# An attention and mixture-of-experts block on one core: rows turned by TensorE in place of DMA transposes, and the diagonal's mask added by VectorE in half of the tiles

## The chip, the core and the metric

The kernel runs on one core of a Trainium2 chip. The metric is the time of one execution on the device in microseconds (us), the median of several runs. TensorE is called PE in the profile, VectorE DVE, ScalarE ACT, GpSimd POOL, and the engine that mostly issues DMAs SP. "Turning" a block of rows is transposing it, so that features lie on partitions, as a matrix product needs them.

## What is computed

The reference takes x of 2 sequences of 2048 tokens with 256 features. All in f32:

```python
mod = silu(c) @ wmod                                  # sa, ca, ga, sb, cb, gb of each sequence
h = layernorm(x) * (1 + ca) + sa
q, k, v = h @ Wq.T, h @ Wk.T, h @ Wv.T                # 2 query heads of 128, one head of keys and values
q, k = apply_rope(q), apply_rope(k)
scores = where(causal, q @ k.T * 128 ** -0.5, -inf)
x = x + ga * ((softmax(scores) @ v) @ Wo.T)           # ga, gb kept away from zero
h = layernorm(x) * (1 + cb) + sb
gate = softmax(h @ Wg + bg); thr = sigmoid(h @ Wt + bt) * 0.125
w = relu(gate - thr); w = w / sum(w)                  # weights of 8 experts
out = x + gb * sum_e w[e] * (gelu(h @ W1[e] + b1[e]) @ W2[e] + b2[e])
```

A token goes only to the experts whose weight is not zero, so how many tokens an expert gets depends on the data.

## The kernel before, in words

**Attention.** The 4096 tokens are 32 tiles of 128 (`tile_steps`), 16 of each sequence, taken in groups of 4, later 2 and 1, from both sequences in turn; r is the tile's number in this order. A tile is loaded (line 505), normalized (516), turned on PE (`turn`, 525), projected to q, k and v (548, 553) and rotated. `score` (600) multiplies a head's q by the keys in chunks of up to 512 columns; the last chunk holds the diagonal, and a second, bf16 product (604) of an identity and a triangular mask is added to it in PSUM. `keep` (611) is one VectorE pass that scales the chunk into SBUF and takes each row's maximum on the way; `top` (618) takes the maximum over the chunks. ScalarE takes the exponentials (627). The probabilities are turned on PE (`turn_p`, ptr, 673), copied out by ScalarE (677) and multiplied by v (pav, 683). After the output projection (717) and the residual sum, `hx` is the second normalization's result. GpSimd splits each f32 of hx into two halves of 16 bits (`halves`, 750), SP writes them to the DRAM table `feats` (759), and in all but the last 4 tiles SP turns them by a DMA transpose of 16-bit elements (`turn_halves`, 771), after which GpSimd or VectorE joins the halves again (`join_halves`, 775). In the last 4 tiles PE turns hx (`turn_h`, 767). A product with the router's weights (787) gives the logits; `gate_steps` forms the weights and the place of each token in its experts' lists.

**The order of attention.** `Plan` holds every step with an engine, an estimated cost, what it comes after, which buffers it takes and gives, and a rank. It plays the steps through and emits each engine's instructions in the order that results. The first steps of a tile (up to the maxima, `lead`) have a rank that is 5 tiles ahead. Each change of a cost, a step or a buffer count can so change the order of all engines. At the start PE runs 8 idle products (312), and `by_feature` (379) makes the shifts and scales of the first normalization by 8 small products.

**Ahead of the experts.** The first 2 items of expert 0 (512 rows) are computed inside attention (1055, 1072, 1079), their rows gathered and turned by `fetch`. Engines then read the token counts into registers (`hold`), PE runs 5 idle products and, behind a barrier, 4 more (1294).

**Experts.** An item is up to 256 tokens of one expert; the last item of an expert can be a half of 128. Items are numbered by t through all experts. Each engine runs its own loop, and semaphores tie them together:

- GpSimd (`item`, 1453): waits until the row buffer xr is free, copies the indices (1441), gathers the item's rows of `feats` by two indirect DMAs (1397); in up to 8 items of an expert it also writes a part of the next expert's list by four indirect DMAs (1413 to 1421); then it adds an earlier item's output to the result by two (1431).
- SP (`turn`, 1233 to 1239): waits for the gather and for xp to be free, and turns xr into xp by one DMA transpose.
- VectorE (`item`, 1338): forms gates, waits until all of item t's h is done, joins xp into xT for item t+1 (`ready`, 1335), adds b2 to y (1363), multiplies by the gate (1374).
- PE (`item`, 1264): waits for xT, makes h in 8 products of two halves each (1272) through HB = 6 PSUM buffers, then y from the 8 gelus (1282).
- ScalarE takes the gelu of each h (1307); at the start of expert e it issues the loads of expert e+2's weights.

b2 of all experts is broadcast to every partition in attention (344).

Of the kernel before, what the change touches and what calls it, by code (L numbers as in the profile page):

```python
# [15 lines left out]
U16 = mybir.dt.uint16  # L16
# [25 lines left out]
HB = 6  # L42
# [68 lines left out]
def adaln_block_kernel(ctx, tc, x, wqkvT, woT, wgt, bgt, w1, b1T, w2, b2, cT, wmod, rope, out):  # L111
# [21 lines left out]

# [16 lines left out]
    b2_bc = const.tile([P, E, D], F32, name="b2_bc")  # L152
    gb_bc = const.tile([P, B, D], F32, name="gb_bc")
    lists = [dram.tile([NTOK, ENT], F32, name=f"list_{e}") for e in range(E)]
    feats = dram.tile([NTOK, 2 * D], U16, name="feats")
# [11 lines left out]
    with tc.manual_schedule():  # L167
        attention(
            tc, x, wqkvT, woT, wgt, bgt, w1, b1T, w2, b2, cT, wmod, rope, out, ident, counts,
            b1_sb, b2_bc, gb_bc, lists, feats, place, entry, weights, wpool,  # L170
            kept,
        )
# [4 lines left out]
    for e in range(RES, E):  # L177
# [3 lines left out]
    xr = ep.tile([P, CI * 2 * D], U16, name="xr")  # L181
    xp = ep.tile([P, CI * 2 * KD, P], U16, name="xp")
# [10 lines left out]
    mcur = ep.tile([P, CI, ENT], F32, name="mcur")  # L193
    to = ep.tile([P, NW], I32, name="to")
    new = ep.tile([P, NW, ENT], F32, name="new")
    hs = [pp.tile([P, TI], F32, name=f"h{z}") for z in range(HB)]
    ys = [pp.tile([P, D], F32, name=f"y{c}") for c in range(CI)]
    experts(
        tc, nc, lists, feats, out.rearrange("b t d -> (b t) d"), counts, ident, b1_sb, b2_bc,
        gb_bc, w1, w2, weights, xr, xp, kept, gs, gate, part, yb, yo_end, who_end, sheets, at, mcur, to, new,  # L200
# [4 lines left out]
def attention(  # L205
    tc, x, wqkvT, woT, wgt, bgt, w1, b1T, w2, b2, cT, wmod, rope, out, ident, counts,
    b1_sb, b2_bc, gb_bc, lists, feats, place, entry, weights, wpool,
# [6 lines left out]
    room = {"ps": 6, "pav": 2, "x": 9, "s": 16, "pT": 3, "hx": 4, "hp": 3, "qT": 3, "big": 3, "xn": 3,  # L214
            "hT": 2, "hT2": 2, "hpT": 2, "aT": 2, "g_sb": 1, "sign": 1, "size": 1}
# [61 lines left out]
    make_causal_mask(nc, maskb, mask_val=MASKED)  # L277
    make_identity(nc, identb)
# [15 lines left out]
    def places_back():  # L294
        nc.vector.tensor_copy(back[:, 0, :], ids)
        for z in (1, 0):
            nc.vector.tensor_scalar(back[:, z, :], back[:, 0, :], float(z - NTOK), None, ALU.add)
# [4 lines left out]
    def load(dst, src, kb, rank=first, **how):  # L302
        return plan.add(
            "SP", max(0.5, kb / 360.0), lambda: nc.sync.dma_start(dst, src), late=2.0, rank=rank,
            **how
        )
# [7 lines left out]
    plan.add("PE", 3.4, lambda: idle_work(8), take=["ps"], give=["ps"], rank=first - 5)  # L314
# [13 lines left out]
    for t0, t1 in [(0, 1), (1, 4)] + [(q, q + 4) for q in range(4, NT, 4)]:  # L328
# [14 lines left out]
    l_b2 = load(  # L343
        b2_bc.rearrange("p e d -> p (e d)"), b2.rearrange("e d -> (e d)").partition_broadcast(P),
        1024, rank=6.0,
    )
# [27 lines left out]

    def by_feature():
        box["pm"] = pm = ps_tile("pm")
        for j in range(2 * KD):
            for k in range(KD):
                nc.tensor.matmul(
                    pm[:, j * B : (j + 1) * B], wm_0[:, k, ts(j, P)], sc[:, k, :],  # L380
                    start=(k == 0), stop=(k == KD - 1),
                )
# [9 lines left out]
    m_pe = plan.add("PE", 2.0, by_feature, after=[s_sc, l_m0], take=["ps"], rank=first)  # L392
# [95 lines left out]
    def tile_steps(b, i, r, group, g):  # L488
# [14 lines left out]
        def load_x():  # L503
# [6 lines left out]
            "SP", 0.5, load_x, late=2.0, take=["x"], rank=first + early[r] if r in early else r  # L510
# [85 lines left out]
        def score(h, c):  # L596
            w = min(SC, n - c * SC)
            st["sc", h, c] = ps = ps_tile(f"psc{u}_{h}_{c}")
            last = c == nch - 1
# [6 lines left out]
        def keep(h, c):  # L606
            w = min(SC, n - c * SC)
            s = st["s", h, c] = work([P, SC], "s", f"{u}_{h}_{c}")
            if ("mx", h) not in st:
                st["mx", h] = little([P, 4], "mx", f"{u}_{h}")  # L610
            nc.vector.tensor_scalar(  # L611
                s[:, :w], st["sc", h, c][:, :w], scale, None, ALU.mult, ALU.max,
                accum_out=st["mx", h][:, c : c + 1],
            )

        def top(h):
            st["nmx", h] = little([P, 1], "nmx", f"{u}_{h}")
            nc.vector.tensor_reduce(  # L618
                st["nmx", h], st["mx", h][:, :nch], AX.X, ALU.max, negate=True
            )  # L620
# [14 lines left out]
        for h in range(NH):  # L635
            kept = []
            for c in range(nch):
                w = min(SC, n - c * SC)
                n_s = lead(
                    "PE", w * 0.00168 + (0.06 if c == nch - 1 else 0.0),  # L640
# [5 lines left out]
                    lead("DVE", 0.1 + w * 0.0013, lambda h=h, c=c: keep(h, c), [n_s], give=["ps"])  # L646
# [101 lines left out]
        def halves():  # L748
            st["hp"] = work([P, 2, D], "hp", u, U16)
            nc.gpsimd.tensor_copy(  # L750
                st["hp"], st["hx"].bitcast(U16).rearrange("p (d two) -> p two d", two=2)
            )


        by_dma = r < NTOK // P - 4
        n_f = add("POOL", 0.65, halves, [n_h], take=["hp"], give=["hx"] if by_dma else [])
        n_hp = add(
            "SP", 0.5,
            lambda: nc.sync.dma_start(
                feats[ts(b * NT + i, P), :], st["hp"].rearrange("p two d -> p (two d)")  # L760
            ), [n_f], late=2.0, give=[] if by_dma else ["hp"],
        )
# [6 lines left out]
        def turn_halves():  # L769
            st["hpT"] = work([P, 2 * KD, P], "hpT", u, U16)  # L770
            nc.sync.dma_start_transpose(st["hpT"], st["hp"].rearrange("p two d -> p (two d)"))

        def join_halves(eng):
            st["hT2"] = work([P, KD, P], "hT2", u)
            of[eng].tensor_copy(
                st["hT2"].bitcast(U16).rearrange("p k (t two) -> p k t two", two=2),
                st["hpT"].rearrange("p (two k) t -> p k t two", two=2),
            )

        def hT2_out():  # L780
            st["hT2"] = work([P, KD, P], "hT2", u)
            nc.scalar.copy(st["hT2"].rearrange("p k t -> p (k t)"), st["ph"][:, :D])
# [14 lines left out]
        if by_dma:  # L797
            n_t = add("SP", 1.3, turn_halves, [n_f, n_hp], late=2.2, take=["hpT"], give=["hp"])
            n_t = add(
                ["POOL", "DVE"], [0.66, 0.58], join_halves, [n_t], take=["hT2"], give=["hpT"]  # L800
            )
        else:
            n_t = add("PE", 0.32, turn_h, [n_h], take=["ps"])
            n_t = add("ACT", 0.38, hT2_out, [n_t, n_f], take=["hT2"], give=["ps", "hx"])
# [171 lines left out]
    def fetch(index, u, after, to, take=(), low=low):  # L976
# [3 lines left out]
        def gather():  # L980
            st["xr"] = work([P, CI * 2 * D], "g_sb", "_r" + u, U16)
            for c in range(CI):
                nc.gpsimd.indirect_dma_start(
                    out=st["xr"][:, ts(c, 2 * D)],
# [5 lines left out]
        def turn():  # L990
            st["xp"] = work([P, CI * 2 * KD, P], "sign", "_p" + u, U16)
            nc.sync.dma_start_transpose(st["xp"], st["xr"])

        def join():
            dst = to().bitcast(U16).rearrange("p k (c t two) -> p c k t two", c=CI, two=2)
            src = st["xp"].rearrange("p (c two k) t -> p c k t two", c=CI, two=2)
            for c in range(CI):
                nc.vector.tensor_copy(dst[:, c], src[:, c])

        n = low("POOL", 2.6, gather, after, late=3.0, take=["g_sb"])  # L1000
        n = low("SP", 0.1, turn, [n], late=3.5, take=["sign"], give=["g_sb"])
        return low("DVE", 0.8, join, [n], take=take, give=["sign"])
# [23 lines left out]
    before_gelu = list(last_exp)  # L1026
    for k in range(AHEAD):
# [40 lines left out]
        def second(c, f0, st=st, k=k):  # L1068
            if (c, f0) == (0, 0):
                st["py"] = ps_tile(f"pya_{k}")  # L1070
            for f in range(f0, f0 + NF // 2):
                nc.tensor.matmul(  # L1072
                    st["py"][:, ts(c, D)], st["g", f // 2 * 2][:, ds(f % 2 * TI + c * P, P)], weights[0][1][:, f, :],
                    start=(f == 0), stop=(f == NF - 1),
                )

        def result(c, k=k, st=st):
            yo = kept.yo[k][:, c, :]
            nc.vector.tensor_tensor(yo, st["py"][:, ts(c, D)], b2_bc[:, 0, :], ALU.add)
# [3 lines left out]
        for f0 in range(0, NF, 2):  # L1083
# [5 lines left out]
            )  # L1089
            n_a.append(low(  # L1090
# [4 lines left out]
        for c in range(CI):  # L1095
            for f0 in (0, NF // 2):
# [3 lines left out]
                    take=["ps"] if (c, f0) == (0, 0) else [],  # L1100
                    give=["s"] * (NF // 2) if (c, f0) == (CI - 1, NF // 2) else [],
                )
            n_r.append(low(
                "DVE", 0.85, lambda c=c, result=result: result(c), [n, n_g, l_b2],
                give=["ps", "size"] if c == CI - 1 else [],
# [29 lines left out]
    def hold(name, eng, columns):  # L1135
        def load():
            kept.count[name] = {at: register(nc, eng, counts, at) for at in columns}
# [4 lines left out]
    low("PE", 2.0, hold("PE", nc.tensor, range(E)), [n_total] + n_ahead)  # L1142
# [20 lines left out]
def experts(  # L1163
    tc, nc, lists, feats, rows, counts, ident, b1_sb, b2_bc, gb_bc, w1, w2, weights, xr, xp, kept,
# [49 lines left out]
    with tc.tile_critical():  # L1214
        names = (
            "read", "loaded", "planed", "ready", "first", "act", "second", "taken", "parted",
            "gated", "copied", "named", "biased", "added", "waited", "paused", "indexed", "staged",
# [4 lines left out]
        with nc.Block() as block:  # L1222

            @block.sync
            def _(sync):
# [7 lines left out]
                def turn(t):  # L1233

                    sync.wait_ge(sem["loaded"], t * (16 * CI))
                    sync.sem_inc(sem["paused"], 1)
                    sync.wait_ge(sem["ready"], t + 1)
                    sync.sem_inc(sem["paused"], 1)
                    sync.dma_start_transpose(xp, xr).then_inc(sem["planed"], 16)

                sync.sem_inc(sem["planed"], 16)
                done, t0 = 1, 0
                for e in range(E):
                    many = items_of(sync, count(sync, e))
                    if e == E - 1:
# [334 lines left out]
```

## Time and profile before

| what | value |
|---|---|
| median of 3 runs | 1622.2 us (1622.19 to 1622.57) |
| the profiled execution | 1622.67 us, of which the span, first to last instruction, is 1620.5 us |
| mean granted TensorE clock | 0.995 |
| h, line 1272 | 2752 PE records, busy 584.9 us |
| y, line 1282 | 2640 PE records, busy 585.8 us |
| ptr, line 673 | 544 PE records, busy 77.1 us, mean 273 ns |
| DMA transposes of items, line 1239 | 86, median 1237 ns in SP's queue |
| stage of the experts | about 464 to 1610 us |

In the rows of the profile a group is "line engine operation out<-in, shapes, xcount", then its busy time and the mean duration of one. PEld is PE's weight load, which runs beside the products. An f32 product stands as two records, a transpose as one. Durations of PE overlap, as its work is pipelined; how much of PE a kind takes is read from the starts of successive records. A timeline row gives the start, the length, the engine, the line and how many instructions were merged. A row of the windows gives a stretch of the span, then for each engine the busy us and the number of instructions, the granted clock of PE, the DMA share and GB/s.

### The profile page before, as it was taken

What the parts mean: (1) busy time and instruction counts of PE and PEld (TensorE: products, weight loads), DVE (VectorE), ACT (ScalarE), POOL (GpSimd) and SP (SyncE); (2) the same over time, 40 slices, a digit from 0 to 9 for tenths busy, and PEclk for the clock granted to TensorE, in tenths of its full rate; (3) what the DMA queues carried; (4) which work ended last, traced back from release to release, by engine and by line L of the source; (5) the groups of instructions that cost most, each with busy time, mean ns of one, the idle gap of its engine ahead of it and who ended that gap; (6) DMA issues with size and microseconds to landing.
All of it is one profiled execution on the core that took longest, in us unless ns stands there. A gap on an engine that the chain in (4) does not pass through costs nothing.

```text
span 1620.5 us, 26414 instructions
## 1 busy us (share of the span) xinstructions
PE 1596.6 (99%) x7916; PEld 1361.7 (84%) x7916; DVE 665.1 (41%) x2141; ACT 588.2 (36%) x1385; POOL 907.2 (56%) x1063
## 2 busy tenths in 40 slices
PE   8999999999999999999999999999999999999997
PEld 6877777777878888888888888888888888888886
DVE  6888767567422332323323222222322232222322
ACT  5576665655522222222222222222222222222322
POOL 5656524222147767757757765664776477534433
PEclk9999999999999999999999999999999999999998
DMA  6511111101033353434345334433533333333333
GB/s 237 155 40 50 40 40 30 30 21 43 20 96 59 67 114 59 67 56 111 57 69 111 59 64 92 78 59 59 110 58 66 60 60 60 62 58 58 62 56 48
DMA packets 181521, 111.10 MB, mean 69 GB/s; under 512 B 126354, under 2 KB 172050, under 8 KB 181332
## 3 DMA queue, kind: packets, MB, share of 16 engines
q0 software_dynamic: 41968, 46.83, 18.0%
q1 hardware_dynamic: 131348, 50.43, 13.6%
q10 hardware_dynamic: 8144, 13.11, 2.4%
q8 instruction: 28, 0.46, 0.1%
q14 instruction: 33, 0.27, 0.1%
HBM read 51.44 MB, written 31.87 MB: 51 GB/s over the span
## 4 chain that ended last, share of the span: by engine, by line
PE 95%; issue 1%; DVE 1%; POOL 1%; ACT 1%; another core or an unknown queue 0%; DMA 0%; SPq 0%; POOLq 0%; DVEq 0%; ACTq 0%
PE h L1272 35%; PE y L1282 34%; PE pav L683 7%; PE psc L600 7%; PE ptr L673 3%; PE pq L548 2%; PE po L717 2%; PE pya L1072 1%; PE pha L1055 1%; PE pq L553 1%; PE pl L787 1%; POOL list L900 0%; PE pt L525 0%; DMA x<-in_x 0%
## 5 line engine op out<-in xcount | busy, mean ns | idle before, releaser
L1307 ACT ACTIVATE g<-h,b_sb 128x256 f32<-128x256 f32 (+1 forms) x688 | 317.5, 465 | 838.5 <-PE h L1272 737.1
L1282 PE MATMUL y<-w,g 128*128 128x256 f32 x2640 | 585.8, 379 | 2.3 <-ACT g L1307 1.9
L1272 PE MATMUL h<-xT,w 128*128 128x256 f32 (+1 forms) x2752 | 584.9, 371 | 0.1
L1272 PEld LDWEIGHTS h<-xT,w 128*128 128x128 f32 x2752 | 506.1, 190 | 66.4 <-DVE xT L1335 0.8
L1282 PEld LDWEIGHTS y<-w,g 128*128 128x128 f32 x2640 | 500.4, 190 | 72.8 <-ACT g L1307 4.2
L1431 POOL DMA_INDIRECT out<-yo,who x172 | 277.0, 1610 | 219.3 <-DVE yo L1374 163.2
L1421 POOL DMA_INDIRECT list<-new,to x216 | 221.7, 1027 | 93.6 <-issue 69.1
L1363 DVE TENSOR_TENSOR yb<-y,b_bc 128x256 f32<-128x256 f32 x165 | 62.7, 420 | 422.7 <-PE y L1282 375.3
L1397 POOL DMA_INDIRECT xr<-feats,at x172 | 171.7, 998 | 100.4 <-POOL at L1441 70.3
L1335 DVE COPY xT<-xp 128x512 uint16<-128x512 uint16 x172 | 68.7, 441 | 315.6 <-PE h L1272 156.6
L600 PE MATMUL psc<-kT,qT 128*128 128x512 f32 (+3 forms) x320 | 144.1, 532 | 0.8 <-DVE thr L853 0.8
L683 PE MATMUL pav<-pT,v 128*128 128x256 f32 x544 | 143.7, 386 | 0.3 <-ACT pT L677 0.3
L683 PEld LDWEIGHTS pav<-pT,v 128*128 128x128 f32 x544 | 96.4, 190 | 38.9 <-issue 21.2
L627 ACT ACTIVATE s<-s,nmx 128x512 f32<-128x512 f32 (+3 forms) x160 | 104.5, 656 | 38.5 <-DVE nmx L618 38.3
L611 DVE TENSOR_SCALAR_CACHE_REDUCE s<-psc 128x512 f32<-128x512 f32 (+3 forms) x160 | 96.8, 608 | 50.8 <-PE psc L600 36.1
L677 ACT COPY pT<-ptr 128x512 f32<-128x512 f32 (+1 forms) x144 | 77.6, 562 | 56.6 <-PE ptr L673 50.2
L900 POOL DMA_INDIRECT list<-entry,place x40 | 41.9, 1048 | 80.9 <-DVE place L897 47.1
L1350 DVE SCALAR_TENSOR_TENSOR gate<-gb_bc,mcur,part 128x256 f32<-128x256 f32 x172 | 77.0, 488 | 3.0
L673 PEld LDWEIGHTS ptr<-ident,s 128*128 128x128 f32 x544 | 64.8, 141 | 15.4 <-issue 5.7
L673 PE MATMUL ptr<-ident,s 128*128 128x128 f32 x544 | 77.1, 273 | 0.0
L1441 POOL COPY at<-sheet 128x2 int32 x85 | 61.7, 725 | 13.3 <-DMA xp<-xr 11.1
L1374 DVE TENSOR_TENSOR yo<-yb,gate 128x512 f32<-128x512 f32 (+1 forms) x85 | 57.2, 673 | 3.9
(171 smaller groups left out, 1076.4 us busy)
## 6 DMA issues: line engine op xcount, KB each, us to landing
w<-in_w ACTq DMA_DIRECT2D x12, 1024.0 KB
x<-in_x SPq DMA_DIRECT2D x32, 128.0 KB, 4.3
w<-in_w SPq DMA_DIRECT2D x4, 1024.0 KB
out<-x SPq DMA_DIRECT2D x32, 128.0 KB, 1.7
feats<-hp SPq DMA_DIRECT2D x32, 128.0 KB, 1.7
list<-new,to POOLq DMA_INDIRECT x216
xr<-feats,at POOLq DMA_INDIRECT x172
out<-yo,who POOLq DMA_INDIRECT x172
```

Of the source, the lines that this page charges most:

```text
L600: nc.tensor.matmul(ps[:, :w], st["qT"][:, h, :], kT[:, ds(c * SC, w)], start=True, stop=not last)
L611: nc.vector.tensor_scalar(s[:, :w], st["sc", h, c][:, :w], scale, None, ALU.mult, ALU.max, accum_out=st["mx", h][:, c : c + 1],)
L627: nc.scalar.activation(s[:, :w], s[:, :w], AF.Exp, bias=st["nmx", h], accum_out=st["den"][:, h, c : c + 1],)
L673: nc.tensor.transpose(ptr[:, j, h, :], s[:, ds((c0 + j) * P % SC, P)], ident)
L677: nc.scalar.copy(pT[:, :m], st["ptr", c0][:, :m])
L683: nc.tensor.matmul(st["pav"][:, : NH * P], v[:, c0 + j, :], st["pT", c0][:, j].rearrange("p h t -> p (h t)"), start=(c0 + j == 0), stop=(c ...
L1272: last = pe.matmul(hs[f % HB][:, :w], weights[e][0][:, k, ts(f, P)], xT[:, k, :w], start=(k == 0), stop=(k == KD - 1),)
L1282: last = pe.matmul(ys[c], gs[f][:, ts(c, P)], weights[e][1][:, f, :], start=(f == 0), stop=(f == NF - 1),)
L1307: act.activation(gs[f][:, :w], hs[f % HB][:, :w], AF.Gelu_apprx_tanh, bias=b1_sb[:, at : at + 1],).then_inc(sem["act"], 1)
L1397: pool.indirect_dma_start(out=xr[:, ts(c, 2 * D)], out_offset=None, in_=feats, in_offset=bass.IndirectOffsetOnAxis(ap=at[:, c : c + 1], ax ...
L1421: pool.indirect_dma_start(out=lists[e], out_offset=bass.IndirectOffsetOnAxis(ap=to[:, j : j + 1], axis=0), in_=new[:, j, :], in_offset=Non ...
L1431: pool.indirect_dma_start(out=rows, out_offset=bass.IndirectOffsetOnAxis(ap=who[:, c : c + 1], axis=0), in_=yo[:, c, :], in_offset=None, c ...
```

## The change

The rows are turned by PE from f32, so neither the halves nor the DMA transposes remain, and `feats` holds whole words.

- In the experts PE's item has a `turn(t + 1)` between h and y: it waits for the gather of item t+1 and turns its four 128x128 blocks into a PSUM tile xt, which takes the place of one h buffer (HB = 5). VectorE copies xt to xT. GpSimd waits for this turn before it gathers into xr again. SP only reads the lists.
- In attention PE turns hx of all tiles, ScalarE or VectorE copies the result, and the write of hx to `feats` is issued behind the turn. `fetch` turns on PE too.
- In tiles with r of 16 or more the mask's product is left out; `keep` handles the diagonal's 128 columns apart: one VectorE instruction scales and adds the mask, another takes the maximum.
- b2 of expert 0 is loaded in attention, that of the others on ScalarE's queue at the start of expert 1; VectorE waits for it there.
- At the start there are 12 idle products, the first shifts and scales come from two 512-column products, a ScalarE copy and four small transposes, with 3 idle products between; x has 12 buffers for 9, and some loads are planned as later. Ahead of the experts the two halves of y have a PSUM tile each, PE reads its registers one by one between products, and 3 idle products stand in place of 4.

```diff
-HB = 6
+HB = 5
+BY_PRODUCT = 16
...
-    feats = dram.tile([NTOK, 2 * D], U16, name="feats")
+    feats = dram.tile([NTOK, D], I32, name="feats")
...
-    plan.add("PE", 3.4, lambda: idle_work(8), take=["ps"], give=["ps"], rank=first - 5)
+    plan.add("PE", 5.0, lambda: idle_work(12), take=["ps"], give=["ps"], rank=first - 5)
...
+    def first_rows():
+
+        pr = box["pr"] = ps_tile("pm")
+        for k in range(KD):
+            nc.tensor.matmul(
+                pr[:B, :], sc[:, k, :], wm_0[:, k, :], start=(k == 0), stop=(k == KD - 1)
+            )
...
+            nc.tensor.transpose(
+                pm[:, j * B : (j + 1) * B], by_row[:, j // KD, ts(j % KD, P)], ident[:B, :B]
+            )
...
-            last = c == nch - 1
+            last = c == nch - 1 and r < BY_PRODUCT
...
+            free = w - P if c == nch - 1 and r >= BY_PRODUCT else w
+            if free > 0:
+                nc.vector.tensor_scalar(
+                    s[:, :free], ps[:, :free], scale, None, ALU.mult, ALU.max,
+                    accum_out=mx[:, c : c + 1],
+                )
+            if free < w:
+                at = c + (free > 0)
+                nc.vector.scalar_tensor_tensor(
+                    s[:, free:w], ps[:, free:w], scale, mask, ALU.mult, ALU.add
+                )
+                nc.vector.tensor_reduce(mx[:, at : at + 1], s[:, free:w], AX.X, ALU.max)
...
-        if by_dma:
-            n_t = add("SP", 1.3, turn_halves, [n_f, n_hp], late=2.2, take=["hpT"], give=["hp"])
-            n_t = add(
-                ["POOL", "DVE"], [0.66, 0.58], join_halves, [n_t], take=["hT2"], give=["hpT"]
-            )
-        else:
-            n_t = add("PE", 0.32, turn_h, [n_h], take=["ps"])
-            n_t = add("ACT", 0.38, hT2_out, [n_t, n_f], take=["hT2"], give=["ps", "hx"])
+        n_t = add("PE", 0.24, turn_h, [n_h], take=["ps"])
+        add(
+            "SP", 0.5, lambda: nc.sync.dma_start(
+                feats[ts(b * NT + i, P), :], st["hx"].bitcast(I32)
+            ), [n_t], late=2.0, give=["hx"],
+        )
+        n_t = add(["ACT", "DVE"], [0.38, 0.42], hT2_out, [n_t], take=["hT2"], give=["ps"])
...
-    low("PE", 2.0, hold("PE", nc.tensor, range(E)), [n_total] + n_ahead)
+
+    for e, n in enumerate(products[-E - 1 : -1]):
+        plan.add("PE", 0.05, hold("PE", nc.tensor, [e]), after=[n_total, n], rank=999.0)
...
+                def turn(t):
+
+                    pe.wait_ge(sem["loaded"], t * (16 * CI))
+                    for c in range(CI):
+                        for k in range(KD):
+                            last = pe.transpose(xt[:, k, ts(c, P)], xr[:, c, ts(k, P)], ident)
+                    last.then_inc(sem["turned"], 1)
...
                         last.then_inc(sem["first"], 1)
+                    turn(t + 1)
                     for f in range(NF):
                         pe.wait_ge(sem["act"], t * NF + (f + 1))
...
+                    if e == 1:
+                        act.dma_start(
+                            b2_rest.rearrange("p e d -> p (e d)"),
+                            b2[1:].rearrange("e d -> (e d)").partition_broadcast(P),
+                        ).then_inc(sem["rest"], 16)
...
-                    for c in range(CI):
-                        last = dve.tensor_copy(dst[:, c], src[:, c])
-                    last.then_inc(sem["ready"], 1)
+                    dve.wait_ge(sem["turned"], t + 1)
+                    dve.tensor_copy(xT, xt).then_inc(sem["ready"], 1)
...
+                    if e == 1:
+                        dve.wait_ge(sem["rest"], 16)
                     dve.wait_ge(sem["second"], t + 2)
...
-                    wait("planed", t * 16)
+                    wait("turned", t)
                     fetch(columns(e, i, skip)[:, :, 2:3], t)
```

## The prediction

> **What bounds the kernel now.** I read the page's busy shares first, then the chain of work that ended last, then the windows by stage, then single stretches of the timeline.
>
> ```profile
> PE 1596.6 (99%) x7916; PEld 1361.7 (84%) x7916; DVE 665.1 (41%) x2141; ACT 588.2 (36%) x1385; POOL 907.2 (56%) x1063
> ...
> PE 95%; issue 1%; DVE 1%; POOL 1%; ACT 1%; another core or an unknown queue 0%; DMA 0%; SPq 0%; POOLq 0%; DVEq 0%; ACTq 0%
> ```
>
> TensorE (PE) is busy for 99% of the span and is 95% of the chain; nothing else reaches 60%. A busy PE need not be a PE at its peak, so the stages come next.
>
> ```profile
> core 0: us, PE busy (x) PEld busy (x) DVE busy (x) ACT busy (x) POOL busy (x), PEclk, DMA share, GB/s
> 7.70:14.50 6.80, 5.36 (x24) 4.76 (x25) 2.75 (x12) 0.85 (x3) 2.97 (x6) 0.50 1.03 358
> 150.00:430.00 280.00, 279.60 (x1522) 215.51 (x1521) 188.35 (x706) 167.87 (x430) 94.14 (x143) 1.00 0.13 35
> 430.00:464.00 34.00, 30.69 (x155) 26.28 (x153) 14.22 (x61) 10.32 (x22) 6.14 (x8) 1.00 0.10 26
> 464.00:1610.00 1146.00, 1143.18 (x5396) 1006.04 (x5394) 340.73 (x943) 317.48 (x688) 716.01 (x756) 1.00 0.39 71
> ```
>
> The expert stage (464 to 1610) leaves PE 2.8 us idle in 1146, at full granted clock. Attention from 150 to 430 leaves it 0.4. Only the start (half clock from 7.7 to 14.5) and the hand-over before 464 have slack. How densely PE's own instructions lie:
>
> ```profile
> 902.81 7.07 PE L1272 MATMUL h<-xT,w 128*128 128x256 f32 x32
> 909.71 7.07 PE L1282 MATMUL y<-w,g 128*128 128x256 f32 x32
> 916.62 7.07 PE L1272 MATMUL h<-xT,w 128*128 128x256 f32 x32
> ```
>
> An item is 32 records of h and 32 of y; each block starts 6.90 or 6.91 us after the last, 0.216 us per record, with no break at the change from h to y. So each instruction put on PE in this stage makes the kernel longer by its own cadence.
>
> **What a TensorE transpose costs.** The kernel already turns probabilities (ptr) on PE in the same form, 128x128 f32:
>
> ```profile
> 420.31 1.03 PE L683 MATMUL pav<-pT,v 128*128 128x256 f32 x4
> 421.18 0.60 PE L673 MATMUL ptr<-ident,s 128*128 128x128 f32 x4
> 421.62 1.03 PE L683 MATMUL pav<-pT,v 128*128 128x256 f32 x4
> ```
>
> Four transposes move the next block by 421.62 - 421.18 = 0.44 us, 0.109 each, and four pav take 0.87 = 4 x 0.216, so changing kinds costs nothing. The mean duration of a ptr in the page is 273 ns, but that is latency: neighbours overlap. The Trainium skill (TensorE: Matmul & The Clock Gate, Part 4: PE-mode transpose) gives about 275 ns for a transpose in a kernel's context and says that the clock gate does not count transposes as busy. Priced so, the 412 transposes added below would cost 113 us; by the cadence of this trace, 45. The duration agrees with the rule (273), the price does not; I take 0.109. The gate has nothing to catch in 0.44 us out of 14. Another rule speaks for the change: VectorE: DVE Perf Modes, Rules for kernel authors, would turn a 128x128 block on TensorE where a PSUM destination is acceptable, by its table 390 ns against 1309 by DMA. Here a DMA transpose costs PE nothing (blocks above unbroken), so that saving is worth 0.
>
> **Expert stage.** The DMA transpose of each item goes, and turn(t+1), four transposes, stands between h and y. 86 items (79 whole, 7 half): 86 x 0.436 = +37.5 us, all on the path. VectorE copies xT once from PSUM (512 columns; nearest row line 611's pass over 512 columns of PSUM, 0.69 us) in place of two copies (0.77 together), with the 6.9 us of y to cover it. One h buffer less (HB 5): product f waits for the gelu of f-5, which takes 0.47 us each against PE's 0.86 per f; cost 0, covered by four products (3.4 us). The broadcast of b2 for experts 1 to 7 (896 KB) is issued on ACT's queue at expert 1, ahead of 2 MB of weights; VectorE waits for it before the first output of expert 1, about 13 us later, with who, yo and the next item queued behind it and PE's next y waiting through "taken". At the 358 GB/s of the window above it needs about 2.6 us: cost 0, 3 if the gathers crowd it.
>
> The new wait matters more: PE now waits for the gather in the middle of an item, where before only a DMA did, and xT was needed half an item later. All of y queues behind that wait, and behind y ScalarE and VectorE. At the start of the stage the gather is late:
>
> ```profile
> 470.91 0.95 POOL L1397 DMA_INDIRECT xr<-feats,at  x1 [0.30 <-issue]
> ...
> 471.13 7.07 PE L1282 MATMUL y<-w,g 128*128 128x256 f32 x32
> ...
> 473.99 15.44 SPq L1239 DMA_TRANSPOSE xp<-xr  x2
> ```
>
> The first y started at 471.13; the rows had landed when SP issued the DMA transpose, at 473.99. PE will stand 2.9 us here, once: +2.9 (1 to 4). In the next items GpSimd's own pace decides:
>
> ```profile
> 900.68 0.81 POOL L1441 COPY at<-sheet 128x2 int32 x1
> 914.15 0.77 POOL L1441 COPY at<-sheet 128x2 int32 x1
> ```
>
> With a part of a list to write GpSimd takes 13.47 us per item, against 13.82 of PE before and 14.25 after. Measured in the same way (SP's issue against y's start) the rows were late by 2.8, 2.5, 2.2, 1.9, 1.7, 1.3 in items 1 to 6 of the old trace; the one stall and 0.44 us per item absorb these. At 900 the second gather is issued at 903.64 and lands about 2.9 later, 3.2 before y. GpSimd now waits for "turned" of the last item before gathering, and the scatter of output is queued behind; that point (896.3 for the fetch at 900.68) lies before where it was anyway. After the short last item of an expert the transpose was issued up to 1.9 us after y's start (four times, 5 us in all); three longer items give back 1.3 each. I take +1 (0 to 5).
>
> **Attention.** The rows h of 28 tiles turn on PE, where 4 did: 56 x 0.109 = +6.1. Three fetches turn on PE: 12 x 0.109 = +1.3. The mask product goes in 16 tiles x 2 heads; successive starts show 0.056 us each: -1.8. Sum +5.6, on the path, since PE idles 0.4 us of 280 there.
>
> Off the path: VectorE adds and reduces the diagonal block, 32 times. Nearest rows: 0.29 us for a 128-column pass of line 611, twice, less 0.13 saved on the longer pass: 0.45 each, 14 us, against 92 us idle between 150 and 430; cover gone, PE would wait in psc for at most these 14. ScalarE gets 28 copies of 128x256 (0.37 each, as aT): 10 us against 112 idle. PSUM room stays six, with one more user; lead work is five tiles ahead. POOL loses 32 splittings (1.0 us) and most joins (0.67), SP 28 DMA transposes; x has 12 buffers. These shorten waits that PE hardly had. The 2.4 us that PE lost at 30.2 to VectorE's xn may go or grow with the new order: 0 (-3 to +4).
>
> **Start and hand-over.** The first rows become two 512-column products (4 records x 0.429 = 1.7 us) where 16 narrow ones stood (1.8), plus a ScalarE copy and four small transposes; with 15 warm-up products in place of 8 PE may keep its clock through 7.7 to 14.5, where 16 records of pq ran at 0.213 in place of 0.112: 1.7 us. The added copy lies beside the ordering of weights: take -1.5 (-2.5 to +1.5). Before 464, PE stood 1.45 us ahead of the idle products (registers read) and 0.5 for VectorE between two halves of pya. Register reads now stand among the products and pya has two tiles: -2.0 (-3.3 to 0). The tail (last y to end, 11 us) is not touched.
>
> **Sum.** 37.5 + 5.6 + 2.9 + 1 - 1.5 - 2.0 = +43.5. The profiled execution took 1622.67 (span 1620.5 and 2.2 around it), 0.5 above the median of 1622.2. So 1622.67 + 43.5 = 1666.2, less 0.5: about 1666.
>
> **Rivals.**
> - *GpSimd becomes the pace* (5%). If the new wait for "turned" puts its 13.5 us in series with a late gather, PE waits in each item with a list part: some 55 items at 1 us give 1720. For it: GpSimd at 716 of 1146 and 0.8 us of margin. Against it: the wait's point lies before its fetch.
> - *A transpose costs its duration* (4%): 412 x 0.273 less what ends as before: +110, about 1733. Against it: the ptr stretches.
> - *PE gives less than counted* (15%): start and hand-over at their best ends and no late gather but the first's low end: 43.1 - 2.5 - 3.3 + 1 - 2 = +36, about 1658.
> - *Not slower* (2%): the matmuls themselves speed up because 86 DMA transposes no longer compete for memory. It decides once the 5168 records of 256 columns fall from 0.216 to 0.2076 us (43.5 / 5168 = 8.4 ns); past that, at 0.207, 1619. Against it: pav of the same form runs at the same 0.216 in attention, where the DMA share is 0.13 and not 0.39. All of PE's waits at start and hand-over together would not do: some 24 us.
>
> The rest, 74%, is the forecast. Adding the high ends of the small terms gives about 1677; with the low case that is the range, 1657 to 1677, leaving out the two dear cases. A measurement can tell about 0.2%, 3.2 us: faster 1%, within 1%, slower 98%.
>
> **What would show it.** In the profile after: PE near x8300 (416 transposes and 14 warm-up records added, 46 records gone), still 99% busy; a row of xt with 344 transposes; items of 14.25 us; y blocks 7.34 us after h; one wait of xt for the gather near 474, and few others; no "issue" of 1.4 us before the stage. The forecast is wrong if items are 13.8 (transposes hidden), or above 14.6 (waiting for the gather), or if attention ends later than 8 us beyond its old end.

## The result, and the profile after

| | before | after |
|---|---|---|
| median | 1622.2 us (4 runs, 1619.18 to 1622.57) | 1670.34 us (4 runs, 1668.35 to 1671.46) |
| ratio to before | | 1.030 (95% interval 1.0282 to 1.0317) |
| profiled execution, its span | 1622.67, 1620.5 us | 1669.68, 1667.8 us |

The change makes the kernel 3% slower. The forecast of 1666 is 4 us short, and the range of 1657 to 1677 held the time. First the busy shares and the chain of the kernel after:

```profile
PE 1643.2 (99%) x8300; PEld 1400.9 (84%) x8300; DVE 656.7 (39%) x2089; ACT 594.6 (36%) x1406; POOL 875.8 (53%) x1023
...
PE 93%; POOL 2%; issue 2%; DMA 2%; DVE 0%; POOLq 0%; another core or an unknown queue 0%; ACT 0%; SPq 0%; DVEq 0%; ACTq 0%
```

PE's busy time grew by 46.6 us and the span by 47.3. What is new in the chain is small: DMA has 2% where it had 0%, "issue" 2% for 1%. GpSimd fell from 56% to 53%, so it has not become the pace. A middle item of the experts, PE's timeline of the kernel after:

```profile
508.10 7.07 PE L1260 MATMUL h<-xT,w 128*128 128x256 f32 x32
515.01 0.60 PE L1249 MATMUL xt<-ident,xr 128*128 128x128 f32 x4
515.45 7.07 PE L1271 MATMUL y<-w,g 128*128 128x256 f32 x32
522.36 0.81 PE L1260 MATMUL h<-xT,w 128*128 128x256 f32 x3
```

h still takes 6.91 us, and y starts 0.44 us after the turn: 0.109 per transpose. From h to h it is 14.26 us, where it was 13.81. The windows of the kernel after show the same for attention (columns as before):

```profile
7.70:14.50 6.80, 5.92 (x51) 5.47 (x51) 3.91 (x13) 2.95 (x7) 3.03 (x6) 1.00 1.03 352
150.00:430.00 280.00, 280.00 (x1526) 216.97 (x1526) 191.06 (x737) 171.62 (x442) 80.41 (x116) 1.00 0.07 23
```

From 150 to 430 PE does not stand at all, with VectorE at 191 us of 280 (188 before) and ScalarE at 172 (168): the mask's adding and the copies are covered. At the start the granted clock is 1.00 where it was 0.50, and 51 PE records fit where 24 did. What is left to look for is in PE's waits (total, times, longest):

```profile
PE xt L1249 <- DMA xr<-feats,at: 4.2, 5, 1.5
PE h L1260 <- issue: 3.3, 1, 3.3
PE y L1284 <- issue: 1.8, 1, 1.8
PE pi L312 <- POOL ident masks.py:199: 1.4, 1, 1.4
PE y L1271 <- ACT g L1297: 1.1, 3, 0.4
```

The first line is the new wait for the gather. The forecast has no term for the second: PE stands once for 3.3 us before an h, waiting for nothing that the profile shows.

**An account of PE's time.** I counted each PE record at the cadence of its kind, as unbroken stretches show it (0.2158 us for 256 columns of f32, 0.109 for a transpose, 0.112 for other f32 records of up to 128 columns, 0.323 for 384, 0.429 for 512, 0.056 for 128 of bf16). The sum is called work, the rest of the time a stall; idle products and what half clock adds count as stalls. "Hand-over" runs from the last product of attention to the first h at the stage's start; behind the last y each kernel has 11.0 us more. All values are us of one profiled execution each; the labels are those of the experiments below.

| run | attention: work | its stalls | hand-over | experts: work | their stalls | span |
|---|---|---|---|---|---|---|
| before | 437.7 | 21.0 | 5.5 | 1140.5 | 4.7 | 1620.5 |
| after | 443.6 | 14.9 | 4.1 | 1178.0 | 16.2 | 1667.8 |
| e8_changed_again | 443.6 | 15.1 | 4.1 | 1178.0 | 16.5 | 1668.3 |
| e1_dma_all | 436.1 | 16.2 | 6.4 | 1140.5 | 2.1 | 1612.4 |
| e2_pe_in_attention | 442.2 | 15.9 | 4.2 | 1140.5 | 1.6 | 1615.5 |
| e3_turned_twice | 443.6 | 15.9 | 4.1 | 1215.5 | 10.7 | 1700.7 |
| e4_turn_mid_y | 443.6 | 15.0 | 4.1 | 1178.0 | 3.6 | 1655.3 |
| e9_mid_y_again | 443.6 | 15.4 | 4.1 | 1178.0 | 11.8 | 1663.8 |
| e10_mid_y_mask_on_tensore | 445.3 | 16.8 | 4.0 | 1178.0 | 9.8 | 1665.0 |
| e5_start_only | 437.9 | 19.6 | 5.5 | 1140.5 | 4.4 | 1619.0 |
| e6_hand_over_only | 437.7 | 19.7 | 4.2 | 1140.5 | 3.5 | 1616.7 |
| e11_x12_b2_only | 437.7 | 19.0 | 5.5 | 1140.5 | 3.6 | 1617.3 |
| e7_mask_on_tensore | 445.3 | 16.0 | 4.1 | 1178.0 | 12.4 | 1666.8 |

The span's +47.3 is so +37.5 of turns in the experts, +11.5 of stalls there, and -1.7 at the stage's start: +5.8 of work in attention against -6.1 of stalls and -1.4 of hand-over. The work columns are counts and measure no cadence by themselves. That is measured by the whole items: their median from h to h is 13.81 us before, 14.25 after and 14.69 in e3, which turns twice.

The chip was not the same for all runs: e1 to e4 ran on one, on which the kernel before took 1618.75 (36 runs), e5 to e8 on a second (1623.9, 30 runs), e9 to e11 on a third (1623.19, 15 runs). Within one of these groups times may be set beside each other; between groups I use the ratio to the kernel before, or the account. The kernel after was not run beside e1 to e4, nor beside e9 to e11.

### The profile page after: what moved, and what is told of

Read it like the earlier page. It is cut to its first block, busy times and chain, and to the rows that moved or that the text cites. A ratio compares the mean times of both kernels' runs of the same rounds, so it can differ in the third digit from the quotient of the medians.

```text
span 1667.8 us, 26340 instructions
## 1 busy us (share of the span) xinstructions
PE 1643.2 (99%) x8300; PEld 1400.9 (84%) x8300; DVE 656.7 (39%) x2089; ACT 594.6 (36%) x1406; POOL 875.8 (53%) x1023
## 2 busy tenths in 40 slices
DMA packets 72449, 84.09 MB, mean 50 GB/s; under 512 B 17154, under 2 KB 62978, under 8 KB 72388
## 4 chain that ended last, share of the span: by engine, by line
PE 93%; POOL 2%; issue 2%; DMA 2%; DVE 0%; POOLq 0%; another core or an unknown queue 0%; ACT 0%; SPq 0%; DVEq 0%; ACTq 0%
PE y L1271 33%; PE h L1260 31%; PE psc L611 7%; PE pav L710 7%; PE ptr L700 3%; PE pq L559 3%; PE xt L1249 2%; PE po L744 2%; DMA xr<-feats,at 2%; PE pq L564 1%; PE pya L1073 1%; PE pha L1056 1%; PE pl L792 1%; POOL out L1426 1%; PE ph L779 0%
## 5 line engine op out<-in xcount | busy, mean ns | idle before, releaser
L1271 PEld LDWEIGHTS y<-w,g 128*128 128x128 f32 x2640 | 494.1, 190 | 68.3 <-ACT g L1297 4.9
L1354 DVE TENSOR_TENSOR yb<-y,b_rest 128x256 f32<-128x256 f32 x148 | 56.2, 420 | 442.0 <-PE y L1271 410.9
L1325 DVE COPY xT<-xt 128x512 f32<-128x512 f32 x86 | 59.5, 692 | 351.7 <-PE xt L1249 317.2
L625 DVE TENSOR_SCALAR_CACHE_REDUCE s<-psc 128x512 f32<-128x512 f32 (+3 forms) x152 | 90.9, 602 | 48.5 <-PE psc L611 45.4
L650 ACT ACTIVATE s<-s,nmx 128x512 f32<-128x512 f32 (+3 forms) x160 | 104.7, 658 | 14.3 <-DVE nmx L641 14.1
L1436 POOL COPY at<-sheet 128x2 int32 x85 | 31.5, 371 | 67.5 <-PE xt L1249 66.1
```

What stands on the lines that cost most here:

```text
L625: nc.vector.tensor_scalar(s[:, :free], ps[:, :free], scale, None, ALU.mult, ALU.max, accum_out=mx[:, c : c + 1],)
L650: nc.scalar.activation(s[:, :w], s[:, :w], AF.Exp, bias=st["nmx", h], accum_out=st["den"][:, h, c : c + 1],)
L1271: last = pe.matmul(ys[c], gs[f][:, ts(c, P)], weights[e][1][:, f, :], start=(f == 0), stop=(f == NF - 1),)
```

## The experiments

**The turn by itself.** My theory is that the loss is the turns' own cadence. First all of the change without its turns (e1), and then with those of attention alone (e2). Both still have the start, the hand-over, the mask, b2 and x's buffers of the kernel after. In e1 the halves and DMA transposes stay everywhere; e2 differs from it by one line:

```diff
-        by_dma = r < NTOK // P - 4
+        by_dma = False
```

> All turning given back to DMA (as before the change), with the rest of the change kept: the start, the hand-over, VectorE's mask, b2 in two loads, 12 buffers of x. My theory (PE's queue is the time; each instruction costs its cadence, and the start and the hand-over gave back 7.3 us): before, less 1.8 for the mask's products, less 7.3: about 1613 (1610 to 1616). Rival (the start and the hand-over became shorter because SP, GpSimd and the DMA queues were relieved of the transposes): within 2 us of before, 1620 to 1622.

> As e1, but attention's rows are turned by PE, as in the change (the experts and the three fetches by DMA). My theory: 56 transposes at 0.109, so 6.1 us above e1, about 1619. Rival (the PE turns shorten the chain to the router and SP's queue, and pay for themselves in waits): equal to e1. With the changed kernel it also gives the price of the experts' part alone: 1670.3 less this, expected 37.5 for the transposes, 1.3 for the fetches and up to 10 for waits and the clock at the stage's start.

Measured: e1 1615.54 us (1613.45 to 1617.34), ratio 0.9974 (0.9967 to 0.9982); e2 1617.13 (1616.3 to 1617.9), 0.9987 (0.998 to 0.9994). So without the turns the change is a small gain, and what makes it slower is in the experts and the three fetches ahead of them. The gain of e1 is 3.2 us where my theory had 9.1, so the theory was too high. e2's work is 6.1 above e1's, as expected, but the median grew by 1.6 and the span by 3.1 only: e1 has a hand-over of 6.4 us where e2 has 4.2. PE's waits in e1:

```profile
PE y L1330 <- issue: 3.5, 1, 3.5
```

These are the idle products behind the barrier ahead of the experts: PE came there earlier than it could go on. Part of attention's turns so falls into this wait; the sum had them all on the path.

In e3 each block is turned twice, so the experts have 344 transposes more and nothing else:

```diff
-                    for c in range(CI):
+                    for c in [*range(CI), *range(CI)]:
```

> The changed kernel with each item's four transposes done twice, so 344 more and no new wait. My theory (0.109 each, in place): +37.5, about 1706 to 1708, a little less where the longer item absorbs a late gather. Rival A (a transpose costs its duration, 0.273): +94, about 1764. Rival B (the cost sits in the waits and in the handshake, not in the transposes): within 5 us of 1670.

Measured: 1699.88 us (1695.62 to 1702.51), ratio 1.0489 (1.047 to 1.0509). The timeline of its PE:

```profile
510.45 7.07 PE L1260 MATMUL h<-xT,w 128*128 128x256 f32 x32
517.36 1.04 PE L1249 MATMUL xt<-ident,xr 128*128 128x128 f32 x8
518.23 7.07 PE L1271 MATMUL y<-w,g 128*128 128x256 f32 x32
525.14 7.07 PE L1260 MATMUL h<-xT,w 128*128 128x256 f32 x32
```

Eight transposes take 0.87 us, twice the 0.44 of four, and an item takes 14.69 us: 0.436 more in each of 86 items is 37.5 us for 344 transposes, 0.109 each. Had a transpose cost its duration of 273 ns, the step would be 94 us; had the cost been in the handshake around the turn, it would be near zero. Both are shown wrong. The span grew by 32.9 and not 37.5, mainly as the experts stalled less (10.7 for 16.2): turning twice gives the gathers 0.44 us more per item to arrive, and two of them were late where five were.

**The wait for the gather.** e4 puts the turn in the middle of y, so that it comes 3.45 us later:

```diff
-                    turn(t + 1)
                     for f in range(NF):
+                        if f == NF // 2:
+                            turn(t + 1)
                         pe.wait_ge(sem["act"], t * NF + (f + 1))
```

> The changed kernel with the turn of the next item after the fourth gelu's products of y and not ahead of y, 3.4 us later, so that a gather has that much longer. My theory (4.2 us of PE's time are waits of the turn for a late gather, and nothing else is lost by waiting): 3 to 4 us less, about 1667. Rival (GpSimd starts a gather only behind a turn, so that a later turn makes the gather as much later): no change, 1670, or worse if the copy of xT then ends too late for h, by up to 1 us per item.

Measured: 1658.28 us (1657.21 to 1659.65), ratio 1.0244 (1.0227 to 1.0261). The waits for the gather are gone, xt has no line among PE's waits, and the stalls of the experts fell to 3.6; the granted clock also stayed at 1.00 through the stage. That was more than the theory gave, and I took the move for a remedy. e9 is the same kernel on another chip:

> The kernel with the turn in the middle of y once more, as the base for the next run. 1658 (1656 to 1661). A stand of PE at the switch from expert 3 to expert 4 of about 3.2 us, as in the run before. If the stand came from chance in the memory system it should be absent or elsewhere this time.

Measured: 1667.68 us (1663.57 to 1671.18), ratio 1.0275 (1.0257 to 1.0294). The ratio of the kernel after in e8 (1.0277, below) is no different, so a gain by the move is not shown. The waits for the gather are gone here as well, but PE's waits name another:

```profile
PE h L1260 <- DVE xT L1326: 3.6, 4, 2.2
PE h L1260 <- issue: 3.3, 1, 3.3
```

After a half item's y there are only 1.7 us between the turn and the next h, too little for VectorE's copy if that starts late. In e9 it did, once by 3 us: PE's and VectorE's timelines of that place,

```profile
1333.98 0.60 PE L1249 MATMUL xt<-ident,xr 128*128 128x128 f32 x4
1334.42 1.89 PE L1272 MATMUL y<-w,g 128*128 128x256 f32 x8
1338.48 1.78 PE L1260 MATMUL h<-xT,w 128*128 128x256 f32 x7 [2.17 <-DVE xT L1326]
```

```profile
1337.73 0.69 DVE L1326 COPY xT<-xt 128x512 f32<-128x512 f32 x1 [5.47 <-remote]
```

xt was there at about 1334.6, VectorE had nothing to do, and the copy started at 1337.73. In e4 the turn of the same item started at 1327.92 and ended 0.44 us later, and the copy followed in 0.2 us:

```profile
1328.56 0.69 DVE L1326 COPY xT<-xt 128x512 f32<-128x512 f32 x1 [2.37 <-PE xt L1249]
```

What held VectorE back the trace does not say ("remote"); it came at the same item in e10, and not on e4's chip. So on this chip moving the turn left waits for the copy of 3.6 and 5.1 us (e9, e10), where the gather's had been 4.2 and 1.5 on others (after, e8).

**The stand before h.** The 3.3 us of "issue" came in the kernel after at the first item of expert 4, while the weights of expert 6 were being loaded; those of expert 4 had been asked for at 738. Expert 3 is the only one without a half item, so this is the one switch at which PE's program jumps over a half item's code. PE's timeline and the DMA queues there (queue: packets, MB, share of 16 engines, from 1025 to 1039):

```profile
1038.30 2.23 PE L1260 MATMUL h<-xT,w 128*128 128x256 f32 x7 [3.28 <-issue]
```

```profile
q10 hardware_dynamic: 1312, 2.10, 46.4%
q8 instruction: 1, 0.02, 0.5%
q14 instruction: 2, 0.02, 0.3%
```

Packets of instructions (q8, q14) were fetched among 2.1 MB of weights (q10); that of q8 ran from 1035.5 to 1036.6, inside the stand. My theory was that PE stands for the fetch of its own next piece of program, and that a longer program ahead of it would move or end the stand. e7 has the mask's product in all 32 tiles again (BY_PRODUCT of 32 for 16), 32 weight loads and products more in attention; it was made for the mask, with the kernel after beside it as e8:

> The changed kernel with the mask's product kept on PE in all 32 tiles (BY_PRODUCT = 32). My theory (32 products of 0.056 on the path): 1.8 us above the changed kernel, and its first h 1.8 later, near 464.3. Rival (the two extra VectorE instructions per head made PE wait as much): no change or less.

> The changed kernel once more, beside the others of this chip. My theory: 1.030 of before, about 1667, and in the trace the same waits of the turns for late gathers at the same items (4 to 5 us), while the stretches of half clock[...] may lie elsewhere. Rival (the gather waits are chance as well): other items.

Measured: e7 1668.9 us (1667.83 to 1669.54), ratio 1.0271 (1.0252 to 1.029); e8 1669.94 (1668.68 to 1670.81), ratio 1.0277 (1.0257 to 1.0296). As expected the stage starts later in e7, by 2.7 us (1.8 of it work), yet the time is no longer. PE's waits of e8, and then of e7 (which has no line of h):

```profile
PE h L1260 <- issue: 3.5, 1, 3.5
PE xt L1249 <- DMA xr<-feats,at: 1.5, 3, 0.8
```

```profile
PE xt L1249 <- DMA xr<-feats,at: 5.0, 5, 2.5
```

The stand of 3.5 us is absent from e7. e10 repeats that, with the same edit made to e9's kernel:

> The same with the mask's product in all 32 tiles, so that PE's program has 32 weight loads and 32 products more ahead of the experts. Theory (the stand at the switch from expert 3 to 4 comes from where a piece of PE's program falls that must be fetched while weights load): the stand of 3.2 us is gone, PE works 1.8 us more, the stage starts about 2.5 later: all in all about 1 us less to 1 us more than the run beside it. Rival (the stand belongs to the switch itself, whatever the program's length): the stand stays and the time is about 1.8 to 2.7 us longer.

Measured: 1666.37 us (1661.03 to 1666.78), ratio 1.0259 (1.0242 to 1.0276), 1.3 below e9 on the same chip, which their runs do not tell apart. PE's waits of e10:

```profile
PE h L1260 <- DVE xT L1326: 5.1, 4, 2.2
PE y L1285 <- issue: 1.8, 1, 1.8
```

Again the stand is gone with the mask's product on PE, though the stage starts 3.2 us later. It was there in all five profiles with a turn in the experts and the mask's product in half of the tiles (after, e3, e4, e8, e9: 3.2 to 3.5 us, on at least three chips), and in neither with the product in all of them. That the edit of the mask takes it away is shown by two pairs of single profiles; why it does is not. The same packets lie at this switch in e10, where PE goes on without a gap (a window of e10, then its queues from 1024 to 1038):

```profile
1034.00:1038.00 4.00, 4.00 (x20) 3.51 (x20) 1.05 (x4) 1.25 (x3) 2.62 (x5) 1.00 1.04 319
```

```profile
q10 hardware_dynamic: 1300, 2.09, 48.5%
q8 instruction: 1, 0.02, 0.4%
q14 instruction: 1, 0.01, 0.1%
```

And e3 has, as its source is written, 32 transposes with their weight loads more ahead of this switch (four in each of the two item bodies of experts 0 to 3), as many as e7's 32 products, and it stood. PE's waits of e3:

```profile
PE h L1260 <- issue: 3.4, 1, 3.4
```

So neither the packets nor the program's length alone makes the stand. The edit also moves the stage's start and takes instructions from VectorE, which was not separated. The cause stays open.

**Where attention's time came back.** The sum gave back 3.5 us at start and hand-over; the account shows 7.5. I took parts of the change alone, on the kernel before: e5 has the new start (12 and 3 idle products, two wide products with copy and small transposes, later loads), e6 the new hand-over (a PSUM tile for each half of y, registers read one by one, 3 idle products), e11 the 12 buffers of x and the split of b2.

```diff
-    plan.add("PE", 3.4, lambda: idle_work(8), take=["ps"], give=["ps"], rank=first - 5)
+    plan.add("PE", 5.0, lambda: idle_work(12), take=["ps"], give=["ps"], rank=first - 5)
...
-                st["py"] = ps_tile(f"pya_{k}")
+                st["py", c] = ps_tile(f"pya_{k}_{c}")
...
-    room = {"ps": 6, "pav": 2, "x": 9, "s": 16, "pT": 3, "hx": 4, "hp": 3, "qT": 3, "big": 3, "xn": 3,
+    room = {"ps": 6, "pav": 2, "x": 12, "s": 16, "pT": 3, "hx": 4, "hp": 3, "qT": 3, "big": 3, "xn": 3,
...
-    l_b2 = load(
-        b2_bc.rearrange("p e d -> p (e d)"), b2.rearrange("e d -> (e d)").partition_broadcast(P),
-        1024, rank=6.0,
-    )
+    l_b2 = load(b2_0, b2[0].partition_broadcast(P), 128, rank=6.0)
```

> The kernel before, with nothing but the change's start: 12 idle products, the first rows by two 512-column products and small transposes, 3 idle products between, later plan times of the first loads (x keeps 9 buffers). In the changed kernel PE loses 6.5 us less than before ahead of the hand-over, where the prediction had 1.5. My theory now (the start is where most of that comes from: full clock from 7.7 on and no wait for xn at 30): 4 to 6 us less than before, about 1613 to 1615 where before is 1618.7. Rival (the start gives its 1.5 to 2 of clock, and the rest comes from GpSimd, SP and the DMA queues having less to do in attention): 1617.

> The kernel before, with nothing but the change's hand-over: registers read between products, a PSUM tile for each half of pya, 3 idle products for 4. My theory: 1.4 us less, as the traces show (5.5 us from the last product to the first h before, 4.1 after): 1617.3. Rival (another engine than PE is last at the barrier, so nothing is gained): 1618.7.

> The kernel before with two parts alone: 12 buffers of x for 9, and b2 loaded for expert 0 only, the rest at the start of expert 1. DMA transposes, mask, start and hand-over stay as before. Theory (these two parts, which the sum priced at 0, carry the rest of what attention gave back): stage starts 2 to 4 us earlier, 1620 where the kernel before has 1623. Rival (the rest came from GpSimd and SP being relieved of halves and joins, or from the mask): no difference, within 1 us of the kernel before.

Measured: e5 1622.17 us (1619.93 to 1624.77), ratio 0.999 (0.9984 to 0.9997), the stage's start 1.2 earlier than in before's profile; e6 1620.82 (1618.64 to 1623.18), 0.9983 (0.9974 to 0.9992), 2.6 earlier; e11 1619.26 (1618.17 to 1620.66), 0.9979 (0.997 to 0.9988), 2.1 earlier. In time they are 1.7, 3.1 and 3.9 us below before on their chips. My theory for e5 of 4 to 6 us falls: the new start is worth 1.2 to 1.7 us, as the prediction had it. e6 gave more than its 1.4, and x's buffers and b2, priced at 0, give 2.1 at the stage's start. Their stalls and hand-overs lie 1.5, 2.6 and 2.1 below before, 6.1 of the 7.5; the other 1.4 (GpSimd and SP without halves, the new order of all engines) were not separated. They also don't add up in time: e1, which has all three and the mask, is not further below before (0.9974) than e11 alone (0.9979) by more than the intervals allow. So e1 and e11 both beat the kernel before and the kernel after, and which is the better is open.

## Why the prediction was right

- **A transpose costs 0.109, not 0.273: right.** Items grew by 0.44 us, which is about 37.5 in all as in the sum, and by as much again in e3. This alone is four fifths of the loss. The rival of the duration (1733) is wrong.
- **First gather, +2.9: right in size, hidden in the profile.** The kernel after lost 1.0 us there, because its first h block ran at half clock for 3.4 us and so came 1.6 later; e3 and e7, without half clock there, lost 2.8 and 2.6.
- **Later gathers, +1 (0 to 5): low.** In the kernel after four cost 1.2, 1.6, 0.6 and 0.5 us, in the first items after an expert's half item: 4.0, the range's upper part. The place is the one named; the size varies, with 1.8 in e8.
- **A stall that the sum did not have: the failed term.** The stand before h cost 3.4 us, and half clock after stands of PE 1.6 and 1.8. The windows of the kernel after:

```profile
462.50:466.00 3.50, 3.50 (x11) 2.78 (x11) 1.67 (x4) 0.48 (x1) 2.89 (x3) 0.52 0.82 322
...
1038.00:1042.00 4.00, 3.70 (x11) 3.05 (x12) 1.29 (x4) 0.95 (x2) 3.21 (x2) 0.68 0.27 33
```

  11 records instead of 16 in 3.5 us. These 6.8 us had no term in the sum. Together with the gathers they make the experts' stalls 16.2, where the sum had the old 4.7 and 3.9 more.
- **Attention +5.6, start -1.5, hand-over -2.0: work right, stalls too small.** +5.8 of work came; 7.5 of stalls and hand-over went, and not 3.5: -1.7 in place of +2.1. The experts' stalls came out 7.6 us above the sum and this part 3.8 below it, so half of the error was taken away again. That is luck: the forecast is nearer than its parts.
- **The range's upper end: added up wrongly.** The high ends that the prediction states for its small terms lie 14.1 us above its sum, which gives 1680 and not about 1677. The time lies below both.
- **HB of 5, VectorE's copy, mask and ScalarE's copies at 0: right.** PE's waits for gelus around half items cost 3.7 us after and 4.3 before; psc and ptr wait 0.8 us in all. e7 bears the mask out from the other side: taking it off PE saved 1.8 us of work. It had no effect on the time that can be told.
- **GpSimd's pace: no.** It waits now for PE's turn, 66 us in 47 items, with time to spare.
- **The faster matmuls: no.** h and y stay at 6.91 us per 32 records with 72449 DMA packets for 181521.

Signs named ahead held: x8300, 344 transposes, items of 14.26, y 7.35 us after h, no 1.4 us of "issue" before pi. "Few other waits" held less well: four of them, 4 us.

## What to carry to other kernels

Here a DMA transpose that landed in time cost a busy TensorE nothing (items of 13.81 us without a break); the same work on TensorE cost its cadence of 0.109 us, read from successive starts and not from durations. Where PE has no gaps, a new wait in its stream is paid in full (5.0 us of gathers here), and at times again as half clock behind it (1.6 to 3 us). A gain or loss in a few stands should be seen on more than one chip before it is put down to an edit: one kernel here was 1.0244 of before on one and 1.0275 on another.

## What was not expected of the hardware

- Late in a stand of PE or just behind it, the granted clock fell to half for 3.4 us (after at 462.6 and 1039.5) or 6.8 (e8 at 1036.6), which takes 1.6 to 3 us of work. The Trainium skill (TensorE: Matmul & The Clock Gate, Part 1: The HAM clock gate) has half clock follow an idle window of about 3.4 us and says that the windows run freely, not from the kernel's start. The lengths agree, and so does e4, which stood for 3.2 us, less than a window, and kept its clock of 1.00. That it takes a whole window of standing does not agree: in e10 the stand below of 1.92 us was followed by a clock of 0.70 over the next 3.4 us, while one of 2.17 us in e9 left it at 1.00. What decides is not shown. PE's timeline and the windows of e10:

```profile
589.83 6.49 PE L1260 MATMUL h<-xT,w 128*128 128x256 f32 x21 [1.92 <-DVE xT L1326]
```

```profile
589.80:593.20 3.40, 3.37 (x11) 2.78 (x12) 0.42 (x1) 0.95 (x2) 2.05 (x3) 0.70 0.98 323
```

- PE stood for 3.2 to 3.5 us where the profile shows nothing that it waits for, at the first item of expert 4 in five profiles, and not in two with the mask's product in all tiles.
